# A four-layer convolution and attention kernel: its body is put into a block with another scheduler

## The chip, the cores and the metric

The kernel runs on one core of one Trainium2 chip. Every number is device time in microseconds (us). The metric is the median of the runs; before the change it is 3769.94 us, over 3 runs from 3769.51 to 3772.02. A separate profiled execution tells what each engine did. The engines are named as the profile names them: PE (TensorE, matmul), PEld (its weight load), DVE (VectorE), ACT (ScalarE), POOL (GpSimd) and SP (SyncE, whose queue issues the transfers here). Every engine works through its own queue in the order in which the program lists it. An instruction that waits holds up all that stand behind it on that engine.

## The reference, cut to what matters

The input is 4 images of 256 channels by 64 x 64, in float32. Four layers follow one another, each with a residual:

```
x = x + L0(gn(x))   # 3x3 convolution, group norm, relu -> xs; softmax attention over all 4096 positions
                    #   (theta, phi, g of 128 channels), 1x1 convolution, group norm * 0.1, + xs
x = x + L1(gn(x))   # linear attention: rmsnorm, q k v, softmax of q and k, 4 heads of 32, 1x1, rmsnorm
x = x + L2(gn(x))   # depthwise 3x3 and 1x1 convolutions whose weights are generated from pooled x
x = x + L3(gn(x))   # 1x1 convolution with a mixture of 4 expert weights, mixed by pooled x
```

`gn` is a group norm without weights. The full attention of L0 is the largest part: a 4096 x 4096 table of exponentials per image.

## The kernel before, in words

One function, `conv_preact_fast`, records all instructions for all four images. Tiles come from pools: the work pool has 7 buffers of 128 x 1024 (`k4`), 5 of 128 x 512 (`k2`), 3 of `pr`, 4 of `u`; the PSUM pool has 4 banks for general use (`bank`), 2 for `pf` and 2 for `acc` (`py` and `pss`). A scheduler then takes the recorded instructions and sets their order on each engine, and with it which instructions of different stages lie beside each other. No order is written out by hand, except that the stages are recorded in the sequence of lines 656 to 669: filter transform, then for each image b the tail of image b-1, the convolution of image b+1, the attention of image b and the projection of image b+1. The last image's tail is recorded last, with nothing beside it.

The stages and their lines:

- `convolve` (307 to 355): the 3x3 convolution in a transformed domain. DVE makes the transformed rows and columns (`down`, `across`, into `ra` and `v`), PE multiplies by filters that SP loads into `u` from DRAM (ps_conv, line 325), DVE adds the results up in `big`. It starts with the group norm of the image (`normalise`, bn_stats at 286) and ends with `smoothed` (296 to 305): statistics, then relu on ACT (304), whose result is also stored in DRAM as `xs_d`.
- `project` (358 to 372): theta and phi (ps_tp, 365) and g (ps_g, 370) for 8 chunks of 512 columns. ACT moves the first two from PSUM to `tpg` (366), DVE the third (372).
- `attend` (374 to 413): 8 tiles q0 to q7 of 512 columns. For each of 16 steps m there are two matmuls pf (387), two exponentials on ACT into `pr` (388), two matmuls py (397) and one addition `tot` on DVE (400 and 402, in the helper at 62). At the end of a tile DVE sums the halves of `tot` (`inv`, 404), PE adds over the partitions (pss, 407), DVE takes the reciprocal (408) and multiplies (`yt`, 412), and SP stores `yt` to `y_d` (413).
- `nonlocal_out` (416 to 442): it loads `yt` again, multiplies by a 1x1 weight (ps_wy, 425), takes a group norm, loads `xs` and `xr`, and adds them (438 and 439, in the helper at 65), with statistics for the next norm (441).
- `linear_attention` (445 to 525) has two loops of 8 chunks. The first goes from a normalised copy `xg` and its squares (453, 455) through a sum of squares (ps_ss, 460), ps_qkv (471), exponentials (473), a softmax of q (478 to 480) and a transpose (483) to a running product (ps_ctx, 487). Line 494 stands between the loops. The second goes from ps_o (510) through an rmsnorm (511 to 518) and transposes (522) to an addition into `big` (523) with statistics (524).
- `generated` (530 to 599): ps_h (545) pools a hidden layer, DVE makes the weights `dk` and `pk`, then 64 tap operations `dw` (587) on DVE, ps_pw (595) and the addition into `big` (597).
- `mixed` (602 to 651): mixes the expert weights, then ps_ex (647) and the store of the output.

All of these work on one `big` and one `xp`. What can lie beside a stage of the tail or of the convolution is therefore the attention of another image: it needs `tpg` alone. At the end of the kernel a check of the value range decides on a branch to a general version (`conv_preact_general`), which isn't taken here.

## Time and profile before

| | us |
|---|---|
| median of 3 runs | 3769.94 |
| lowest, highest | 3769.51, 3772.02 |
| profiled execution, its own time | 3772.22 |
| profiled execution, span from first to last instruction | 3770.4 |
| TensorE clock granted in it, mean | 0.912 |
| images 1 to 3, from the end of q6 of one image to that of the next | 907 |
| last tail, with nothing beside it, from the last pss to the end | 423 |

In the tables of stretches, a line gives a stretch of time (from:to in us), its length, and for each engine its busy time with the number of instructions. A float32 matmul shows as two instructions there, and counts as one in the text. The granted clock is 1.00 where the throttle lets TensorE run at full speed. The "chain" is followed back from the last instruction, at each step to what released it. By its lines it runs through pf (20%) and py (20%), ps_conv (9%) and the taps `dw` (8%).

### The profile page before, as it was taken

What the parts mean: (1) busy time and instruction counts of PE and PEld (TensorE: products, weight loads), DVE (VectorE), ACT (ScalarE), POOL (GpSimd) and SP (SyncE); (2) the same over time, 40 slices, a digit from 0 to 9 for tenths busy, and PEclk for the clock granted to TensorE, in tenths of its full rate; (3) what the DMA queues carried; (4) which work ended last, traced back from release to release, by engine and by line L of the source; (5) the groups of instructions that cost most, each with busy time, mean ns of one, the idle gap of its engine ahead of it and who ended that gap; (6) DMA issues with size and microseconds to landing.
All of it is one profiled execution on the core that took longest, in us unless ns stands there. A gap on an engine that the chain in (4) does not pass through costs nothing.

```text
span 3770.4 us, 24367 instructions
## 1 busy us (share of the span) xinstructions
PE 3150.8 (84%) x8322; PEld 1498.2 (40%) x8322; DVE 2208.6 (59%) x2696; ACT 1125.4 (30%) x2111; POOL 88.9 (2%) x133
## 2 busy tenths in 40 slices
PE   4699999989956889998984879999897699967645
PEld 2254444445422334444531334445452244434412
DVE  8869344353697944436479773444567734452476
ACT  2122333335410033333540013333443033323220
POOL 0000000001000000000100000000010000000000
PEclk9899999999977999999996889999998799987667
DMA  5313000020012220001001230000101200020011
GB/s 184 124 35 104 24 6 3 9 73 1 1 52 80 64 90 3 6 20 59 1 26 54 80 117 3 6 9 23 51 1 40 83 6 6 9 67 6 0 31 51
DMA packets 84484, 151.20 MB, mean 40 GB/s; under 512 B 8960, under 2 KB 46592, under 8 KB 82176
## 3 DMA queue, kind: packets, MB, share of 16 engines
q1 hardware_dynamic: 84352, 149.57, 11.6%
q8 instruction: 68, 1.11, 0.1%
q14 instruction: 64, 0.52, 0.0%
HBM read 101.30 MB, written 48.23 MB: 40 GB/s over the span
## 4 chain that ended last, share of the span: by engine, by line
PE 66%; DVE 21%; issue 7%; ACT 3%; POOL 2%; DMA 0%; SPq 0%; POOLq 0%; ACTq 0%; DVEq 0%
PE pf L387 20%; PE py L397 20%; PE ps_conv L325 9%; DVE dw L65 8%; PE ps_ex L647 3%; PE ps_tp L365 3%; DVE big L65 3%; PE ps_qkv L471 2%; PE ps_h L545 2%; PE ps_g L370 1%; PE ps_wy L425 1%; DVE z L62 1%; ACT junk L515 1%; DVE st L598 1%; PE ps_o L510 1%
## 5 line engine op out<-in xcount | busy, mean ns | idle before, releaser
L388 ACT ACTIVATE pr<-pf 128x512 f32<-128x512 f32 x1024 | 604.6, 596 | 1437.8 <-PE pf L387 1105.9
L62 DVE TENSOR_TENSOR tot<-tot,pr 128x1024 f32<-128x1024 f32 x448 | 547.9, 1223 | 826.1 <-ACT pr L388 825.7
L387 PE MATMUL pf<-tpg 128*128 128x512 f32 x2048 | 989.3, 605 | 22.7 <-ACT pr L388 22.7
L397 PE MATMUL py<-pr,tpg 128*128 128x512 f32 x2048 | 976.9, 600 | 11.1 <-DVE ev L62 7.7
L387 PEld LDWEIGHTS pf<-tpg 128*128 128x128 f32 x2048 | 385.7, 193 | 508.8 <-issue 419.1
L397 PEld LDWEIGHTS py<-pr,tpg 128*128 128x128 f32 x2048 | 390.6, 193 | 489.4 <-issue 471.7
L325 PE MATMUL ps_conv<-v,u 128*128 128x512 f32 x768 | 351.1, 618 | 88.3 <-issue 48.5
L595 PE MATMUL ps_pw<-dw,pk 128*128 128x512 f32 x256 | 158.8, 773 | 194.8 <-DVE dw L65 170.6
L65 DVE SCALAR_TENSOR_TENSOR dw<-xp,dk,dw 128x1008 f32<-128x1008 f32 (+1 forms) x256 | 309.9, 1262 | 6.4 <-ACT dw L582 6.2
L325 PEld LDWEIGHTS ps_conv<-v,u 128*128 128x128 f32 x768 | 151.2, 199 | 285.1 <-issue 239.4
L471 PE MATMUL ps_qkv<-wqkv_s,xg 128*128 128x384 f32 x512 | 190.3, 529 | 0.0
L595 PEld LDWEIGHTS ps_pw<-dw,pk 128*128 128x128 f32 x256 | 60.3, 250 | 292.0 <-DVE dw L65 187.4
L328 ACT COPY one<-ps_conv 128x512 f32<-128x512 f32 x48 | 28.1, 586 | 364.9 <-PE ps_conv L325 352.3
L408 DVE RECIPROCAL inv<-pss 128x512 f32<-128x512 f32 x32 | 107.4, 3356 | 42.9 <-PE pss L407 42.9
L471 PEld LDWEIGHTS ps_qkv<-wqkv_s,xg 128*128 128x128 f32 x512 | 103.6, 208 | 68.1 <-issue 16.0
L62 DVE TENSOR_TENSOR s<-sq 128x512 f32<-128x512 f32 x32 | 22.2, 692 | 182.5 <-ACT sq L455 182.5
L365 PE MATMUL ps_tp<-big,wtpg_s 128*128 128x512 f32 x256 | 118.9, 605 | 4.1 <-ACT big L304 4.1
L647 PE MATMUL ps_ex<-big,wm 128*128 128x512 f32 x256 | 119.2, 626 | 0.0
L202 PE MATMUL pm<-mv,avg 128*128 128x2 f32 x48 | 10.1, 279 | 127.8 <-DVE mv L198 96.6
L62 DVE TENSOR_TENSOR v<-ra 128x1024 f32<-128x1024 f32 x96 | 114.4, 1218 | 0.3
L62 DVE TENSOR_TENSOR tpg<-ps_g,bg_s 128x512 f32<-128x512 f32 x32 | 22.1, 690 | 118.1 <-PE ps_g L370 118.1
L138 POOL TENSOR_TENSOR rstd<-rstd,half 128x2 f32<-128x2 f32 x24 | 18.6, 773 | 3057.7 <-DVE rstd L212 3057.7
(176 smaller groups left out, 2679.3 us busy)
## 6 DMA issues: line engine op xcount, KB each, us to landing
u<-filters SPq DMA_DIRECT2D x192, 128.0 KB, 2.3
xp<-in_x_dram SPq DMA_DIRECT2D x16, 1024.0 KB, 5.1
xs_d<-big SPq DMA_DIRECT2D x32, 512.0 KB, 3.0
xs<-xs_d SPq DMA_DIRECT2D x32, 512.0 KB, 6.1
xr<-in_x_dram SPq DMA_DIRECT2D x32, 512.0 KB, 5.3
out_dram<-res SPq DMA_DIRECT2D x64, 256.0 KB, 2.0
y_d<-yt SPq DMA_DIRECT2D x32, 256.0 KB, 2.0
yt<-y_d SPq DMA_DIRECT2D x32, 256.0 KB, 2.9
```

What stands on the lines that cost most here:

```text
L62: nc.vector.tensor_tensor(o, a, b, op)
L65: nc.vector.scalar_tensor_tensor(o, a, s, b, op0, op1)
L325: nc.tensor.matmul(ps, u[:, h, :], vs[k][:, bass.ts(h, 512)], start=(h == 0), stop=(h == NH - 1))
L365: nc.tensor.matmul(ps, wtpg_s[:, h, k, :], big[:, h, cols], start=(h == 0), stop=(h == NH - 1))
L387: nc.tensor.matmul(pf, phi[:, bass.ts(2 * m + s, P)], theta[:, cols], start=True, stop=True)
L388: nc.scalar.activation(pr[:, bass.ts(s, 512)], pf, AF.Exp)
L397: nc.tensor.matmul(py, g[:, bass.ts(2 * m + s, P)], pr[:, bass.ts(s, 512)], start=(m == 0 and s == 0), stop=(m == NM - 1 and s == 1))
L408: nc.vector.reciprocal(inv, pss)
L471: nc.tensor.matmul(ps[:, 0:3 * HID], xg[:, h, bass.ts(j, P)], wqkv_s[:, h, :], start=(h == 0), stop=(h == NH - 1))
L545: nc.tensor.matmul(ps[0:2 * R, :], w1n[:, h, :], big[:, h, bass.ts(c, 512)], start=(h == 0), stop=(h == NH - 1))
L595: nc.tensor.matmul(ps, pk[:, h * NH * P + oh * P:h * NH * P + (oh + 1) * P], dw[h][:, bass.ts(s, 512)], start=(h == 0), stop=(h == NH - 1))
L647: nc.tensor.matmul(ps[oh], wm[:, h, bass.ts(oh, P)], big[:, h, cols], start=(h == 0), stop=(h == NH - 1))
```

## The change

The call of the fast body is put into a block that is asked to schedule by stepping through a model of the chip's timeline. The default scheduler orders everything outside of it, as it did for the whole before. The pools, their buffers, the recorded instructions and the sequence in which they are recorded stay the same. What changes is the order on each engine's queue and which buffer of a pool a tile gets.

```
@@ -1175,7 +1175,8 @@
     B = args[0].shape[0]
     gp = ctx.enter_context(tc.tile_pool(name="guard", bufs=1))
     guard = gp.tile([P, 2, B * NQ + 1], F32, name="guard")
-    conv_preact_fast(tc, guard, *args)
+    with tc.block(name="fast", schedule_with_timeline_sim=True):
+        conv_preact_fast(tc, guard, *args)
 
 
     fit = gp.tile([P, 2, B * NQ + 1], F32, name="fit")
```

In the built programs the orders of PE, DVE, ACT and SP differ over most of their length. In the steady part of the attention the order on PE was pf pf py py and is pf py pf py.

More of the change, by code (lines that the diff above doesn't have):

```diff
@@ L1177, in conv_preact_kernel @@
     guard = gp.tile([P, 2, B * NQ + 1], F32, name="guard")
-    conv_preact_fast(tc, guard, *args)
+    with tc.block(name="fast", schedule_with_timeline_sim=True):
+        conv_preact_fast(tc, guard, *args)
     fit = gp.tile([P, 2, B * NQ + 1], F32, name="fit")
```

## The prediction

> **What bounds the kernel now.** I read the page first (span, busy shares, the chain that ended last), then cut the period of one image into its stages and asked for the busy time of each engine in each, then the same for the last image, whose tail runs with nothing beside it, and last two short timelines.

> ```profile
> span 3770.4 us, 24367 instructions
> PE 3150.8 (84%) x8322; PEld 1498.2 (40%) x8322; DVE 2208.6 (59%) x2696; ACT 1125.4 (30%) x2111; POOL 88.9 (2%) x133
> PE 66%; DVE 21%; issue 7%; ACT 3%; POOL 2%; DMA 0%; SPq 0%; POOLq 0%; ACTq 0%; DVEq 0%
> ```

> TensorE carries two thirds of the chain, VectorE a fifth: the bound changes by stage. The busy table by stretch (columns: stretch, length, busy us and count of PE, PEld, DVE, ACT, POOL, granted clock, DMA share, GB/s), second image:

> ```profile
> 711.80:767.80 56.00, 56.00 (x131) 24.47 (x131) 23.72 (x20) 20.76 (x36) 0.00 (x0) 1.00 0.03 10
> 767.80:816.30 48.50, 48.50 (x197) 28.41 (x197) 18.68 (x24) 18.45 (x30) 0.00 (x0) 1.00 0.14 44
> 816.30:865.20 48.90, 31.21 (x73) 13.83 (x71) 41.28 (x64) 12.28 (x20) 1.45 (x3) 0.79 0.29 97
> 865.20:949.00 83.80, 83.56 (x346) 51.86 (x345) 27.90 (x49) 50.52 (x109) 9.35 (x15) 1.00 0.00 1
> 949.00:1026.20 77.20, 70.60 (x247) 39.46 (x247) 59.91 (x88) 28.75 (x92) 8.75 (x9) 1.00 0.00 1
> 1026.20:1150.90 124.70, 72.11 (x138) 25.34 (x137) 108.30 (x120) 26.52 (x39) 0.00 (x0) 0.78 0.17 57
> 1198.20:1319.10 120.90, 90.17 (x195) 38.76 (x195) 113.06 (x125) 11.74 (x16) 0.70 (x1) 0.86 0.19 58
> 1319.10:1393.80 74.70, 61.16 (x147) 28.15 (x148) 34.04 (x47) 25.75 (x37) 0.70 (x1) 0.89 0.28 111
> ```

> In order: the last attention tile q7 of an image (65 matmuls, 56.00/65 = 0.861 us each, PE full); `project` and ps_wy (full); the residual of `nonlocal_out` (PE idles 17.7 us, DVE 84% busy); the first loop of `linear_attention` (full); its second loop; `generated` (DVE-bound); `convolve` (DVE-bound); the rest of attention tiles q1 and q2. The same stages of the last image, bare:

> ```profile
> 3368.90:3410.80 41.90, 2.07 (x9) 1.85 (x9) 34.19 (x57) 3.15 (x4) 1.45 (x3) 0.54 0.34 113
> 3410.80:3514.10 103.30, 87.02 (x292) 57.57 (x292) 18.75 (x41) 43.62 (x95) 8.44 (x15) 0.76 0.00 1
> 3514.10:3596.80 82.70, 41.73 (x135) 32.97 (x136) 44.91 (x73) 14.56 (x65) 8.75 (x9) 0.64 0.00 0
> 3596.80:3719.10 122.30, 59.66 (x102) 19.90 (x102) 101.01 (x108) 23.10 (x32) 0.00 (x0) 0.70 0.08 24
> ```

> To see here: the second loop (82.7 against 77.2) and `generated` (122.3 against 124.7) take about as long bare as with attention matmuls between. Attention put there costs almost nothing; put where PE is full, it costs 0.861 us a matmul. One chunk of the first loop, from ps_qkv to ps_qkv, with attention between (9.96 us) and bare (12.30 us):

> ```profile
> 897.82 5.41 PE L471 MATMUL ps_qkv<-wqkv_s,xg 128*128 128x384 f32 x16
> 907.78 5.41 PE L471 MATMUL ps_qkv<-wqkv_s,xg 128*128 128x384 f32 x16
> 3426.51 7.29 PE L471 MATMUL ps_qkv<-wqkv_s,xg 128*128 128x384 f32 x16
> 3438.81 6.67 PE L471 MATMUL ps_qkv<-wqkv_s,xg 128*128 128x384 f32 x12
> ```

> **The change part by part.** No instruction of the computation is added or removed; only the order on each engine's queue changes, and the queues run in order. I counted the attention matmuls (pf and py) by stage in the instruction orders of the two built programs, per image. Before: project and ps_wy 0, residual 31, first loop 25, second loop 56, `generated` 18, up to ps_ex 6: 136. After: 24, 62, 48, 0, 0, 0: 134. So 80 matmuls leave stages that hide them, and 78 of these go into the stages ahead, and 24 ps_tp and 48 ps_g matmuls of `project` move up between q7's.

> Working, us per image, second and third image (batches 1 and 2):
> - q7, project, ps_wy: before 56.0 + 48.5 = 104.5, full. After, PE alone: 56.0 + 24 x 0.861 (ps_tp) + 48 x 0.22 (ps_g; from 48.5 less 42 x 0.861 over 56) + 24 x 0.861 + 16 x 0.861 = 121.8. Bounds +17 (nothing waits) and +22 (py waits at two tile ends). Taken: +18.5.
> - Residual: 48.9 before. After, PE 62 x 0.861 + 0.9 (pss) = 54.3 is the floor. DVE has 34.2 bare, plus 13 tot adds x 1.22, inv 0.7 and the reciprocal 3.36: 54.2; the bare chain has 7.7 idle besides: 62. On PE six py (5.2) now stand between the reciprocal and the group norm's second matmul, and everything of the first loop waits for that: upper end 68. Taken 62, for the stage is nearest to the bare row: +13.
> - First loop: without its 25 attention matmuls it is 83.8 - 21.5 = 62.3 on PE, 7.8 a chunk. After, the chunks hold 12, 10, 10, 9, 5, 1, 0, 0 of the 48 (the last one follows). Five PE-bound chunks: 5 x 7.8 + 46 x 0.861 = 78.6; three chain-bound ones at 9.96 to 12.30, taken 11.2: 33.6; end 4.1 (83.8 - 8 x 9.96): 116. Floor is PE alone, 62.3 + 41.3 = 103.6; upper end 120. +32.
> - Second loop bare: 82.7 by the last image, less if the 13.4 us of tot adds that leave DVE were in its way (64). Taken 81, nearer to the row that is the same work: +4.
> - `generated`: 122.3 for 124.7: -2.4. DVE now finishes pk 30 taps later, so ps_pw starts later, but DVE, which bounds the stage, has the same list to do. Up to mixed's first ps_ex 12.3 for 18.9: -6.6. ps_ex at the lower clock 31 for 28.4: +2. `convolve` has no attention in either order, and DVE bounds it: 0 (-3 to +3).
> - From convolve's end to the end of q2: before 74.7 with 61 of PE, because py and ps_tp wait behind smoothing. After, 22 pf and py are placed in that gap, so some 24 us to the first ps_tp as before, then the rest of the stage's 62.1 of PE (60 attention matmuls, 8 ps_tp, 16 ps_g), 62.1 - 20.7 = 41.4: 66, -9 (-12 where smoothing is quicker, -5 where it is not).
> Sum +51.5. The last interleaved image (batch 3) has no convolve, and its gap before ps_ex is bare already: 18.5 + 13 + 32 + 4 - 2 - 2 = +63.5.

> Elsewhere. Steady tiles (56.0): yt now stands behind the next tile's first tot on DVE. The order's waits say that the next py waits for the count that the reciprocal raises, not for yt; 0, upper end 24 tiles x 1.22 = 29. First convolve: 16 bn_stats of the next image (0.6 each) now stand ahead of the last t adds: +5 of these 10. The last tail has the same PE order: 0. On SP's queue the y_d and xs transfers change places with u loads, which run four ahead: 0 to +10, taken 0. POOL's order is unchanged but for memsets at the start.

> Total 2 x 51.5 + 63.5 + 5 = 171.5. On the profiled execution (span 3770.4, own time 3772.2) that makes a span of 3942; the median of the runs is 2.3 under that execution's time, so **3941**.

> A rule that speaks against this order: the granted clock was 1.00 in the filled second loop and 0.64 in the bare one, where ps_o's mean went from 379 to 588 ns. [...]

> **The rivals.**
> 1. Floors (3827): the chains don't matter, each stage ends at PE's own sum. 17 + 5.4 + 20 - 9 - 2.4 - 6.6 - 12 = +12.4 twice, and +31 for the last: +56. For: PE is at 100% in many stretches. Against: the residual and three bare chunks have chains that the last image shows.
> 2. New waits (3985): pf and py alternate one by one and the pools' releases decide; yt's 29 and some 15 more in `project` inside q7, where each ps_tp needs a bank freed by ACT after pf has read phi. Against: pf runs two to eight ahead.
> 3. Not slower (3770 or below): the bare stages shorten. The last image's bare stages from the second loop to ps_ex hold 135 us of PE at a clock of 0.64 to 0.90; at 1.00 they would hold some 36 less (41.7 x 0.36, 59.7 x 0.30, 31.4 x 0.10). If all that lay on the path, with the three chunks at 9.96 (-4), the residual at its floor (-8) and q2 at its best (-3), each image gets 51 back and the change costs nothing. It decides from a clock of about 1.00 in the bare stages. Against: the clock sank in every stretch where PE idled (0.54 to 0.79).
> 4. That nothing changes: excluded, the orders differ on every engine.

> **How the numbers follow.** Main case 0.62, rival 1 0.16, rival 2 0.14, rival 3 0.08. The range from 3860 to 4005 leaves out rival 3 and half of rival 1, and holds the upper ends of single terms. Within 0.2% is what a measurement of this kernel can't tell from no change; slower 0.92, same 0.02, faster 0.06.

> **What would show it.** Right: stretches of q7 of 87 us; about 62 from the last ps_wy to the first ps_ss; a first loop near 116; a second loop and `generated` without pf or py, near 81 and 122, at a clock under 0.8; steady tiles still 56.0; PE's busy time about the same and its idle time some 170 us longer. Wrong: if the bare stages shrink by more than 10 us each, or steady tiles lengthen, or if `convolve` or the first 430 us move by more than 15.

## The result and the profile after

The changed kernel takes 3959.79 us (median of 3 runs, 3959.01 to 3964.73), the kernel before 3769.94. The ratio is 1.0505, with a 95% interval of 1.0484 to 1.0525: slower, 19 us above the 3941 forecast. The profiled execution has a span of 3957.2 us, 186.8 more than before. The page of the changed kernel, in the parts that answer to those of before:

```profile
span 3957.2 us, 24425 instructions
PE 3174.8 (80%) x8322; PEld 1528.6 (39%) x8322; DVE 2213.0 (56%) x2696; ACT 1133.7 (29%) x2111; POOL 86.6 (2%) x133
PE 28%; DVE 11%; issue 2%; ACT 2%; POOL 1%; DMA 0%; SPq 0%; ACTq 0%; POOLq 0%; DVEq 0%
```

TensorE is busy 24 us longer than before, VectorE as long as before. So 163 of the 187 us are time in which TensorE stands still. (The chain's shares add up to under a half here, so nothing is read from it.) The busy table by stretch, second image, cut at the same landmarks as before (columns: stretch, length, busy us and count of PE, PEld, DVE, ACT, POOL, granted clock, DMA share, GB/s):

```profile
711.70:799.00 87.30, 87.30 (x276) 44.45 (x275) 27.78 (x28) 28.24 (x48) 0.00 (x0) 1.00 0.04 13
799.00:833.50 34.50, 34.50 (x81) 14.95 (x80) 20.99 (x23) 16.55 (x29) 0.00 (x0) 1.00 0.15 46
833.50:904.60 71.10, 59.75 (x136) 25.76 (x135) 54.32 (x74) 20.89 (x35) 1.45 (x3) 0.93 0.19 67
904.60:1014.60 110.00, 104.73 (x389) 61.67 (x387) 31.10 (x51) 57.90 (x120) 8.44 (x15) 0.98 0.00 1
1014.60:1096.40 81.80, 40.75 (x136) 32.12 (x137) 45.29 (x73) 14.58 (x65) 8.75 (x9) 0.68 0.00 0
1096.40:1226.20 129.80, 53.05 (x102) 17.95 (x101) 107.11 (x118) 23.19 (x32) 0.00 (x0) 0.69 0.16 54
1273.70:1386.80 113.10, 87.54 (x196) 37.70 (x195) 109.99 (x122) 11.72 (x16) 0.69 (x1) 0.91 0.19 61
1386.80:1461.10 74.30, 65.96 (x174) 30.94 (x174) 36.02 (x51) 27.52 (x40) 0.70 (x1) 0.93 0.30 113
```

In order: q7 with the early part of `project` and 12 attention matmuls; the rest up to the last ps_wy; the residual; the first loop; the second loop; `generated`; `convolve`; and the rest of q2. The residual has 136 TensorE rows where it had 73, and the first loop 389 where it had 346. The second loop fell from 247 to 136 and `generated` from 138 to 102, at a clock of 0.68 and 0.69. So the attention matmuls went where the orders of the two programs said, and the two stages that are left bare take 81.8 and 129.8 us, against 77.2 and 124.7 with the matmuls in them. A steady tile is still 56.0 us (pss at 430.8, 486.8, 542.8).

Time by stage, from the landmarks in the two traces, against the terms of the sum (us, second / third image):

| stage | before | after | measured | forecast |
|---|---|---|---|---|
| q7, project, ps_wy | 104.5 / 105.4 | 121.7 / 121.7 | +17.2 / +16.3 | +18.5 |
| residual, to the first ps_ss | 48.8 / 48.4 | 71.1 / 70.7 | +22.3 / +22.3 | +13 |
| first loop, to the first ps_o | 84.0 / 83.9 | 110.0 / 109.9 | +26.0 / +26.0 | +32 |
| second loop, to the first ps_h | 77.0 / 77.0 | 81.8 / 81.9 | +4.8 / +4.9 | +4 |
| generated, to the last ps_pw | 124.7 / 123.8 | 129.8 / 129.8 | +5.1 / +6.0 | -2.4 |
| to the first ps_ex | 18.9 / 20.3 | 16.4 / 16.0 | -2.5 / -4.3 | -6.6 |
| ps_ex | 28.4 / 30.1 | 31.1 / 31.3 | +2.7 / +1.2 | +2 |
| convolve and on to the end of q2 | 195.6 / 194.8 | 187.4 / 187.1 | -8.2 / -7.7 | -9 |
| sum | 682.0 / 683.8 | 749.4 / 748.4 | +67.4 / +64.6 | +51.5 |
| last interleaved image, q6 to q2 | 541.6 | 611.8 | +70.2 | +63.5 |
| up to q6 of the first image | 711.8 | 711.7 | -0.1 | +5 |
| last tail, q6 to the last ps_ex | 471.7 | 456.4 | -15.3 | 0 |

### The profile page after: what moved, and what is told of

It reads as the page before. It is cut to its first block, busy times and chain, and to the rows that moved or that the text cites. A ratio compares the mean times of both kernels' runs of the same rounds, so it can differ in the third digit from the quotient of the medians.

```text
span 3957.2 us, 24425 instructions
## 1 busy us (share of the span) xinstructions
PE 3174.8 (80%) x8322; PEld 1528.6 (39%) x8322; DVE 2213.0 (56%) x2696; ACT 1133.7 (29%) x2111; POOL 86.6 (2%) x133
## 5 line engine op out<-in xcount | busy, mean ns | idle before, releaser
L397 PE MATMUL py<-pr,tpg 128*128 128x512 f32 x2048 | 1035.5, 601 | 26.0 <-DVE gm L204 13.3
L387 PE MATMUL pf<-tpg 128*128 128x512 f32 x2048 | 1038.2, 598 | 20.7 <-ACT pr L388 20.7
L595 PE MATMUL ps_pw<-dw,pk 128*128 128x512 f32 x256 | 144.1, 723 | 286.4 <-DVE pk L65 234.8
L471 PE MATMUL ps_qkv<-wqkv_s,xg 128*128 128x384 f32 x512 | 190.8, 523 | 0.0
L522 PE MATMUL ps_zt<-ident,z 128*128 128x128 f32 x256 | 62.2, 424 | 144.5 <-DVE z L62 144.5
L471 PEld LDWEIGHTS ps_qkv<-wqkv_s,xg 128*128 128x128 f32 x512 | 101.9, 204 | 71.2 <-issue 20.9
L515 ACT ACTIVATE junk<-z 128x256 f32<-128x256 f32 x128 | 52.0, 407 | 227.4 <-DVE z L62 227.4
L522 PEld LDWEIGHTS ps_zt<-ident,z 128*128 128x128 f32 x256 | 50.2, 223 | 162.0 <-issue 143.0
L510 PE MATMUL ps_o<-w,xp 128*128 128x256 f32 x256 | 102.2, 571 | 1.9 <-ACT w L501 1.9
```

The costliest lines, as they stand in the source:

```text
L387: nc.tensor.matmul(pf, phi[:, bass.ts(2 * m + s, P)], theta[:, cols], start=True, stop=True)
L397: nc.tensor.matmul(py, g[:, bass.ts(2 * m + s, P)], pr[:, bass.ts(s, 512)], start=(m == 0 and s == 0), stop=(m == NM - 1 and s == 1))
L471: nc.tensor.matmul(ps[:, 0:3 * HID], xg[:, h, bass.ts(j, P)], wqkv_s[:, h, :], start=(h == 0), stop=(h == NH - 1))
L510: nc.tensor.matmul(ps[:, j, :], qT[:, bass.ts(4 * c + 2 * s + j, P)], w2, start=True, stop=True)
L522: nc.tensor.transpose(pt[:, bass.ts(j, P)], z[:, j, bass.ts(h, P)], ident)
L595: nc.tensor.matmul(ps, pk[:, h * NH * P + oh * P:h * NH * P + (oh + 1) * P], dw[h][:, bass.ts(s, 512)], start=(h == 0), stop=(h == NH - 1))
```

## The experiments

Two questions were open. Is it the place of the attention matmuls that costs, or are it waits that the new orders of VectorE and ScalarE bring? And why does the new order spend them early and then have none for the second loop?

### What a matmul costs in each stage, by itself

Both runs add to the changed kernel 56 matmuls of pf's shape per image in images 0 to 2. Nobody reads their product; every other result is as before.

```
 second loop, after the chunk's last ps_o                first loop, after the chunk's last ps_ctx
+    more = bank("more")                                 +    more = bank("more")
+    with tc.issue_after(last.ins):                      +    with tc.issue_after(last.ins):
+        for _ in range(7):                              +        for _ in range(7):
+            nc.tensor.matmul(more, ident, ...)          +            nc.tensor.matmul(more, ident, ...)
```

(`issue_after` sets an order on the engine's queue and adds no wait.)

> The changed kernel with extra work that nobody reads: in each chunk of the second loop of images 0 to 2, behind its last ps_o, seven more matmuls of pf's shape (128x512), 56 for an image, 168 in all, 168 x 0.861 = 145 us of TensorE at full clock. This measures by itself what a matmul costs in the stage that the change left bare. Theory P: nothing, since TensorE was busy 41 of 82 us there and is at 28.6 us of work at full clock: 28.6 + 48.2 = 77 us fit into the stage, so it stays between 75 and 86 us and the kernel between 3945 and 3975. Rival (work added to the stage lengthens its chain): up to 145 us, 4105.

> The changed kernel with the same extra work that nobody reads as in the run on the second loop (seven matmuls of 128x512 a chunk, 56 for an image, 168 in all, 145 us at full clock), but in the first loop of images 0 to 2, behind each chunk's last ps_ctx. Theory P: the stage is full there, so a matmul costs its 0.861 us, but for the last three chunks, which had room for some 3 us each: 48 - 8 = 40 us for an image, 3960 + 120 = 4080, between 4050 and 4110; the same work cost nothing in the second loop. Rival (a matmul costs the same wherever it stands): 3941, as there.

Measured: 3941.39 us with the work in the second loop (ratio to the kernel before 1.0460, 1.0443 to 1.0478), 18 us less than without it; and 4096.53 us with it in the first loop (1.0860, 1.0844 to 1.0877), 137 us more. The second loop with the added work, and the first loop with it, second image, from the busy tables of the two runs:

```profile
1017.50:1095.10 77.60, 72.41 (x249) 42.34 (x250) 43.25 (x73) 14.83 (x65) 8.75 (x9) 0.96 0.00 1
```

```profile
906.30:1062.20 155.90, 150.97 (x501) 82.06 (x499) 31.10 (x51) 58.07 (x120) 8.44 (x15) 1.00 0.00 1
```

In the second loop TensorE goes from 40.75 to 72.41 us of work, the granted clock from 0.68 to 0.96, and the stage gets shorter, from 81.8 to 77.6 us: at the higher clock its own ps_o and transposes are faster (means of 408 and 273 ns for 571 and 424; in the kernel before, 379 and 276 in the filled stage at a clock of 1.00, 588 and 424 in the bare one at 0.64), and the added ones lie in its gaps. The kernel lies 4 us below the range that theory P gave, since I had not forecast that the work would gain anything. In the first loop the same 56 matmuls cost 155.9 - 110.0 = 45.9 us, 0.82 us each. So the same work costs less than nothing in one stage and its full duration in the other; the last three chunks of the first loop had hardly any of the room that I gave them. This is theory P, that the place sets the price, in its plainest form.

### The counts by stage put back, or taken over

The first run holds the attention matmuls of images 1 to 3 in the changed kernel, so that each stage has the count of before. The second makes the mirror in the kernel before.

```
+PLAN = (('W', 31), ('s0', 3), ..., ('o0', 7), ..., ('h0', 4), ...)   # behind which matmul, how many
 ...
+    with held(b):      # tc.issue_after(the matmul that PLAN names)
         nc.tensor.matmul(pf, ...)
```

```
+PLAN = (('W0', 24), ('W', 62), ('s0', 12), ('s1', 10), ('s2', 10), ('s3', 9), ('s4', 5), ('s5', 2))
         for q in range(NQ):
+          with tc.high_priority() if (b > 0 and q < 2) else nullcontext():
```

> The changed kernel, its scheduler kept, but each early attention matmul (pf, py) of images 1 to 3 is queued on TensorE behind a named matmul of the other image's tail, so that the counts by stage become the ones of before: 31 in the residual, 25 in the first loop, 56 in the second loop, 18 in generated, 6 up to ps_ex (changed: 24 ahead of the last ps_wy, 62, 48, 0, 0, 0). Theory P (the place of these matmuls is the loss): the three interleaved images give back what they lost, 67.4 + 64.6 + 69.1 = 201 us, and the last tail keeps its 15 us of gain: 3960 - 201 = 3759, between 3745 and 3790. Rival W (the orders that the new scheduler gave VectorE and ScalarE, and the waits in them, are the loss): 3900 or more, since those orders stay. Half each would be 3860. Profile under P: second loop near 77 us with the clock near 1.00, residual near 49.

> The mirror: the kernel before, its default scheduler kept, but the first two attention tiles of images 1 to 3 are given priority over the tail, and their matmuls are queued so that they stand where the changed kernel has them: 24 among the ps_wy, 62 in the residual, 50 in the first loop, none from the second loop to ps_ex. Theory P: the three images lose 201 us as in the changed kernel, and the last tail stays as before: 3770 + 201 = 3971, between 3940 and 3995 (it lies a little above the changed kernel, which has 15 us of gain in its last tail). Rival W: the default order of VectorE and ScalarE is kept, so 3770 to 3820.

Measured: 3885.01 us (1.0299, 1.0282 to 1.0316), and 4089.20 (1.0845, 1.0827 to 1.0863). Neither theory was right: the first run gives back only 75 us, the mirror loses 319 and not 201. In the mirror the residual takes 94.2 us and the first loop 125.8, against 71.1 and 110.0 in the changed kernel with the same counts. The stages of the first run tell more. The residual is back at 51.8 us and q7 to the last ps_wy at 106.6, but the first loop takes 108.5 with its 25 matmuls (84.0 in the kernel before, also with 25), and `generated` 142.9 with its 18. TensorE's work in one chunk of the first loop, kernel before:

```profile
887.86 5.41 PE L471 MATMUL ps_qkv<-wqkv_s,xg 128*128 128x384 f32 x16
893.10 0.83 PE L487 MATMUL ps_ctx<-v,qk 128*128 128x129 f32 x6
893.77 1.02 PE L387 MATMUL pf<-tpg 128*128 128x512 f32 x2
894.63 0.39 PE L487 MATMUL ps_ctx<-v,qk 128*128 128x129 f32 x2
894.86 1.88 PE L397 MATMUL py<-pr,tpg 128*128 128x512 f32 x4
896.57 0.60 PE L483 MATMUL ps_qt<-ident,qk 128*128 128x128 f32 x4
```

and with the counts put back, but behind ps_ss (start, length; in brackets the idle time ahead and what ended it):

```profile
912.21 1.54 PE L487 MATMUL ps_qkv<-wqkv_s,xg 128*128 128x384 f32 x4
913.58 1.88 PE L413 MATMUL py<-pr,tpg 128*128 128x512 f32 x4
915.30 1.02 PE L402 MATMUL pf<-tpg 128*128 128x512 f32 x2
916.15 4.03 PE L487 MATMUL ps_qkv<-wqkv_s,xg 128*128 128x384 f32 x12
920.02 0.83 PE L503 MATMUL ps_ctx<-v,qk 128*128 128x129 f32 x6
921.01 0.49 PE L503 MATMUL ps_ctx<-v,qk 128*128 128x129 f32 x2 [0.15 <-ACT v L490]
922.58 0.63 PE L499 MATMUL ps_qt<-ident,qk 128*128 128x128 f32 x4 [1.08 <-DVE qk L63]
```

In the kernel before three matmuls stand between ps_ctx and ps_qt, just where TensorE would wait for VectorE's softmax of q, and no wait is left. Three matmuls some microseconds earlier in the same chunk delay ps_qkv by 2.6 us, and the wait of 1.08 us for `qk` stays. In `generated` of the same run, 15 of them stand among the ps_h or right behind them, ahead of ps_pool, on which `pk` and then every ps_pw depend. From the first ps_h to ps_pool 29.6 us pass, against 18.1 in the changed kernel and 15.7 in the kernel before, and the stage is 13 us longer than in the changed kernel. TensorE's long wait for `pk` doesn't come from these matmuls: it is as long in the changed kernel, where none stand in this stage (the run, then the changed kernel; total, times, longest):

```profile
PE ps_pw L611 <- DVE pk L66: 58.2, 1, 58.2
```

```profile
PE ps_pw L595 <- DVE pk L65: 58.7, 1, 58.7
```

In the kernel before the first ps_pw starts 19 us behind ps_pool, in the other two 59 to 60: that is VectorE's new order, in which `pk` comes late.

So a count by stage is too coarse. A matmul was free here in a gap of the chain, not in a stage that has gaps: with 25 of them in both, the first loop took 84.0 us in the kernel before and 108.5 in this run.

### TensorE's and VectorE's whole order exchanged

The next four runs therefore take over orders whole: a table of the other kernel's order, as runs of (first, count) in recorded sequence, tied to the engine's queue with no wait added.

```
+PE_ORDER = ((0, 199), (298, 2), (199, 1), (300, 14), ...)     # 4354 matmuls
+DVE_ORDER = (...)                                             # 2660 instructions, in the last two runs
+    row = [made[k] for at, n in order for k in range(at, at + n)]
+    for a, b in zip(row, row[1:]):
+        tc.add_manual_dep(b, a.name, <no sync>, reason="order")
```

> The changed kernel with every matmul of TensorE's queue, all 4354, put into exactly the order that the kernel before has (issue order only, no wait added); the timeline scheduler then orders VectorE, ScalarE and the transfers around it. The run that moved only counts by stage gave back 75 of 201 us, and its first loop (108.5 us) still held waits of ps_qt for VectorE: its 25 attention matmuls stood behind ps_ss and not, as in the kernel before, in the gap between ps_ctx and ps_qt. Theory P2 (the place to the single matmul is the loss): 3755 to 3785, the first loop near 84 us and full. Rival W (the orders of VectorE and ScalarE): like that run, 3860 to 3900.

> The mirror: the kernel before, default scheduler, with all 4354 matmuls of TensorE's queue in exactly the order of the changed kernel; the default scheduler orders VectorE, ScalarE and the transfers around it. Theory P2: 3960 to 3985 (the changed kernel's time, and up to 15 us more where the last tail is without its gain), residual near 71, first loop near 110, second loop near 82 us. Rival W: 3850 or less.

> The changed kernel with both TensorE's order (4354 matmuls) and VectorE's order (2660 instructions) of the kernel before; ScalarE and the transfers are left to the timeline scheduler. With TensorE's order alone it took 3808, 37 us above the kernel before, 10 of them in generated in each image. Theory V (the rest is VectorE's order, which no longer fitted TensorE's): 3760 to 3780. Rival (the rest is on ScalarE or the transfers): 3800 or more.

> The mirror: the kernel before with both TensorE's and VectorE's order of the changed kernel. With TensorE's order alone it took 4070, 110 us above the changed kernel (residual 81 to 85 us for 71, the stretch behind convolve 91 for 74). Theory V: 3945 to 3980, the changed kernel's time. Rival (ScalarE or the transfers): 4030 or more.

| kernel | us | ratio to the kernel before |
|---|---|---|
| changed, TensorE's order of before | 3807.96 | 1.0093 (1.0076 to 1.0110) |
| changed, TensorE's and VectorE's of before | 3782.67 | 1.0030 (1.0019 to 1.0040) |
| before, TensorE's order of the changed | 4069.65 | 1.0790 (1.0772 to 1.0808) |
| before, TensorE's and VectorE's of the changed | 4004.67 | 1.0624 (1.0608 to 1.0640) |

TensorE's order alone gives back 152 of the 190 us, twice what the counts gave; with the matmuls in their gaps the first loop is full again:

```profile
875.10:960.70 85.60, 84.72 (x346) 52.75 (x347) 27.87 (x48) 49.97 (x109) 8.45 (x15) 1.00 0.00 1
```

VectorE's order gives back 25 more. The other way round, TensorE's order makes all of the loss and 110 us besides, and VectorE's order takes 65 of these away: the residual goes from 81.1 to 70.9 us, the changed kernel's value. So rival W is right in this: an order on one engine cost extra where the other engine's queue wasn't ordered for it, 65 us in this case. None of the four met its range: the runs with TensorE's order alone lie 23 and 85 us above that of P2, the last two 3 and 25 us above that of V. What is left, 12 us one way and 45 the other, has to be on ScalarE, POOL, the transfers or the buffers that the tiles got; no run parts these. Of the 45, 12 lie before the end of the first image's q6, 12 and 11 in the next two images, mostly behind `convolve` (84 us for 74), 13 in the last tail, and -3 in the third image. Only the last tail has runs of its own.

### The last tail

It was forecast at 0, since TensorE's order in it is the same, and became 15 us shorter, nearly all in the first loop of `linear_attention`. The prediction shows its busy line of before (103.30 us, TensorE 87.02 at a clock of 0.76). After:

```profile
3612.50:3701.20 88.70, 75.60 (x292) 49.35 (x292) 19.38 (x41) 43.49 (x95) 8.44 (x15) 0.88 0.00 1
```

The same 292 rows of TensorE took 87.02 us and then 75.60, at another clock. What differs is ScalarE's order: before, the two `xg` and `sq` of the next chunk stood one by one between the exponentials of this one, after, they stand ahead of most of them. Two runs of the kernel before test that, one with the last tail in a block, one with priority for these two lines.

```
+    with tc.block(name="last", schedule_with_timeline_sim=True):
         tail(B - 1)
```

```
+    with tc.high_priority() if b == 3 else nullcontext():
         xg ... activation(xg[:, h, :], ...); activation(sq, xg, AF.Square)
```

> The kernel before with only its last tail, which has nothing beside it, in a block of the timeline scheduler. In the changed kernel this tail took 409 us against 423 of before with the same order on TensorE, nearly all of it in the first loop of linear_attention (88.6 against 103.3 us, granted clock 0.88 against 0.76). Theory A (the order on ScalarE does it: xg and sq of the next chunk stand ahead of most of this chunk's exponentials): 3770 - 15 = 3755, plus 0 to 5 for the block's border. Rival (a chance of the clock's phase, carried in from the tiles ahead, which were a little shorter in the changed kernel): 3770, the first loop near 103.

> The kernel before with xg and sq of the last image's first loop given priority, so that on ScalarE they stand ahead of most of the chunk's exponentials, nearly as the timeline scheduler put them; nothing else of the program is touched. In the run with the last tail alone in a timeline block the first loop fell from 103.3 to 94.2 us, and the block's border took 9.2 us back. Theory A (ScalarE's order does it): first loop 88 to 95 us, kernel 3755 to 3763. Rival (it is not ScalarE's order): 3770.

Measured: the block gives 3770.06 (0.9996, 0.9987 to 1.0006): its first loop is 94.2 us instead of 103.3, but from the end of q6 to the last ps_wy it takes 87.0 instead of 77.8. At the block's border every load of `yt` is issued behind the last tile's store, and the first ps_wy waits 7.8 us for one. The priority gives 3760.95 (0.9972, 0.9961 to 0.9982):

```profile
3410.50:3503.60 93.10, 80.65 (x291) 52.46 (x291) 19.38 (x41) 43.61 (x95) 8.44 (x15) 0.81 0.00 1
```

Its loop is 10.2 us shorter and the kernel 10 us, and in its profile TensorE and VectorE work through the whole kernel in the same order as before: ScalarE's order is shown as the cause of two thirds of the 15 us. The block's run, at 3770, has the time that the rival forecast, but not the loop near 103 that went with it. The other runs' last tails settle the rival, that the shorter loop is a chance of the clock. In all of them TensorE's and VectorE's orders in this loop are those of the kernel before. The five programs that also keep its order on ScalarE take 100.0 to 103.3 us for the loop, the nine in which the two `xg` stand together 87.9 to 94.2. Programs of one kind differ by up to 6 us, so the last third of the 15 us lies within that spread. The waits tell how small the first step is. TensorE's wait for the softmax of q in the kernel before and in the changed one (total, times, longest):

```profile
PE ps_qt L483 <- DVE qk L62: 12.1, 8, 2.9
```

```profile
PE ps_qt L483 <- DVE qk L62: 10.2, 8, 2.4
```

2 us less waiting there, and 11 us less time in the matmuls, at a clock of 0.88 for 0.76.

### Why there is nothing left for the second loop

In both programs, 134 to 136 attention matmuls stand ahead of the end of `convolve`: two tiles (128) and the start of a third. Something stops the third. An attention tile ends by taking two tiles of `k2` (`junk` and `yt`), and `convolve`, recorded ahead of it, takes `k2` tiles for `one` to its very end. The trace shows the first early tile held there. In the kernel before its reciprocal starts at 963.8 us, but its `junk` and `yt` run 350 us later, `junk` right behind the last `one`:

```profile
1313.99 0.59 ACT L328 COPY one<-ps_conv 128x512 f32<-128x512 f32 x1 [6.59 <-PE ps_conv L325]
1314.48 0.63 ACT L410 ACTIVATE junk<-inv 128x512 f32<-128x512 f32 x1
1327.88 0.63 DVE L62 TENSOR_TENSOR yt<-py,inv 128x512 f32<-128x512 f32 x1
```

In the changed kernel the reciprocal starts at 884.5, the last `one` at 1381.8, `junk` at 1382.3 and `yt` at 1383.9. Until its `yt` has read it, the first tile's py holds one of the two `acc` buffers, and the second tile's py has the other, so the second tile can't take its pss; that runs at 1329.4 in the one and 1391.2 in the other. Two runs write junk and yt over the tile's own `inv` instead, one of the kernel before, one of the changed kernel.

```
-            junk = k2("junk")
-            nc.scalar.activation(junk, inv, AF.Copy, accum_out=...)
-            yt = k2("yt")
-            tt(yt, py, inv, ALU.mult)
-            nc.sync.dma_start(out=y_d[b, :, cols], in_=yt)
+            nc.scalar.activation(inv, inv, AF.Copy, accum_out=...)
+            tt(inv, py, inv, ALU.mult)
+            nc.sync.dma_start(out=y_d[b, :, cols], in_=inv)
```

> The kernel before with one change of buffers: the accumulating copy and y (junk, yt) of an attention tile are written over its own inv and no longer take two tiles of the k2 buffers that the tail and convolve share. In both orders only 134 to 136 attention matmuls, two tiles and the start of a third, stand ahead of convolve's end. Theory L (that limit is yt, whose k2 tile comes in recorded order behind the last tile of convolve): with it gone the order has 14 for 6 ahead of ps_ex, and 46 more between ps_ex and the end of convolve, where TensorE has room. 46 x 0.861 = 40 us leave the stretch behind convolve in images 1 and 2, less 46 x 0.305 = 14 us of tot adds in a VectorE-bound stage and 5 ahead of ps_ex: -20 twice, -10 for the last: 3720, between 3690 and 3750. Rival (VectorE is the bound there, so nothing is gained): 3760 to 3790.

> The changed kernel with the same change of buffers. Under theory L the timeline scheduler spent its 134 matmuls early and then had none left for the second loop and generated; with the limit gone its order has them everywhere: per image some 85 up to the last residual matmul, 82 in the first loop, 112 in the second, 62 in generated, 38 ahead of ps_ex, 40 around ps_ex and 66 in convolve, some 480 of 512. TensorE's full-clock work for one image and its tail is 448 (attention) + some 290 = 740 us, against 907 of before and 973 of the changed kernel, and VectorE's some 560. Theory L: 800 to 860 an image, so 3960 - 2 x 130 - 90 = 3610, between 3450 and 3700. Rival (the in-order queues wait on the exponentials wherever attention stands in a tail's chain, or VectorE's 1.22 us adds delay the chain): 3770 or more.

Measured: 3657.90 us with the default scheduler (0.9698, 0.9682 to 0.9715), and 3499.02 us with the timeline scheduler (0.9277, 0.9261 to 0.9292): 271 us less than the kernel before, 461 less than the changed kernel. The page of the latter, and its first loop, second loop, `generated` and `convolve`:

```profile
span 3497.0 us, 24215 instructions
PE 3100.9 (89%) x8322; PEld 1483.5 (42%) x8322; DVE 2195.8 (63%) x2696; ACT 1126.1 (32%) x2111; POOL 87.8 (3%) x133
```

```profile
889.90:1027.70 137.80, 137.80 (x475) 76.85 (x474) 50.27 (x67) 70.67 (x142) 8.43 (x15) 1.00 0.01 2
1027.70:1140.40 112.70, 112.70 (x350) 59.00 (x348) 78.28 (x104) 46.48 (x121) 8.75 (x9) 1.00 0.01 5
1140.40:1291.60 151.20, 119.78 (x229) 45.52 (x228) 129.73 (x139) 38.88 (x65) 0.00 (x0) 0.84 0.15 49
1390.70:1530.80 140.10, 140.10 (x328) 62.11 (x327) 124.70 (x134) 27.27 (x47) 0.00 (x0) 1.00 0.19 60
```

(The residual ahead of them is 66.8 us.) Each of these four stages is longer than in either kernel, and the image is shorter: from the last ps_wy of one image to that of the next, 907 us before and 973 in the changed kernel have become 809 and 806, of which TensorE works 773 at a clock of 0.97. Theory L holds: the limit was the buffer. With the default scheduler and the new buffers the second early tile's pss runs at 1164.8 us instead of 1329.4. (That the buffers of a tag go out in the recorded sequence is my reading of it; shown is that the limit goes when these two tiles leave `k2`.) With the default scheduler the gain was 114 us, twice the forecast and beyond its range: the period fell by 41 us an image, which is all of 46 x 0.861 = 40; the 14 us that I took off for VectorE's additions were not lost.

This turns the meaning of the change round. With enough attention to lay beside the tail, the timeline scheduler is 159 us better than the default one (3499 against 3658). With two tiles of it, it is 190 us worse, because it uses them as soon as TensorE can take them, and TensorE can take them first where each one costs 0.86 us.

## Why the prediction was right, and where it was off

The direction and the main mechanism, the place of the attention matmuls, were right, and so was the size: 3960 for 3941. The size owes something to luck: the three interleaved images lost 36 us more than forecast, and the last tail and the start gave 20 of them back. By its own steps:

- **The counts by stage carry the loss.** Right as a forecast: the three images lost 202 us for 166 forecast. As a cause it was too coarse, which only the runs showed: the counts put back gave 75 us, TensorE's whole order 152, and VectorE's order 25 more.
- **q7, project, ps_wy (+18.5).** +17: nothing waited, the stretches are full at a clock of 1.00.
- **Residual (+13).** This step failed: +22, beyond the upper end of 68 us. VectorE's busy time was forecast at 54.2 and measured at 54.3. The miss is in "the bare chain has 7.7 idle besides". In the bare tail 6.8 us pass from the group norm's first matmul to the first ps_ss; here 21.6. VectorE's reciprocal stands ahead of the copy of `gm`, then six py ahead of pv:

```profile
882.99 0.28 PE L202 MATMUL pm<-mv,avg 128*128 128x2 f32 x2
884.52 3.35 DVE L408 RECIPROCAL inv<-pss 128x512 f32<-128x512 f32 x1
887.78 0.10 DVE L204 COPY gm<-pm 128x2 f32<-128x2 f32 x1
887.92 8.00 PE L397 MATMUL py<-pr,tpg 128*128 128x512 f32 x12 [4.65 <-DVE gm L204]
895.75 0.28 PE L210 MATMUL pv<-ev,avg 128*128 128x2 f32 x2
```

  I had named these six py and priced them at 5.2; behind TensorE's wait of 4.65 us the clock was 0.67 and they took 8.0, and ten more pf and py stand between pv and ps_ss.
- **First loop (+32).** +26, between the floor of 103.6 and the upper end of 120.
- **Second loop (+4).** +5. What the prediction held against this order, the lower clock of the bare stage, came: 0.68, with 40.75 us of TensorE's work in a stage of 81.8. The 28.6 us that the run on this loop was forecast with, as the stage's work at full clock, is shown by no run: in the filled stage of the kernel before (949.0 to 1026.2, clock 1.00) ps_o and ps_zt hold 15.1 + 8.6 = 23.7 us. The run with useless work in the gaps puts a number on the clock: at 0.96 the stage takes 77.6, so the lost clock is worth about 4 us of it, as an estimate from these two times.
- **generated (-2.4) and on to ps_ex (-6.6).** Wrong by some 8 and 3 us. I took the bare row of the last image, 122.3, but that image has no successor: in the second and third, 12 bn_stats of the next image's norm, 0.68 us each, stand in VectorE's list of this stage (118 instructions, 107.1 us busy, against 108 and 100.9 in the last). The third tail, which has no next image to normalise either, took exactly 122.3. These bn_stats make the forecast wrong, but they don't make the stage 5 us longer: the kernel before has 11 of them there too. Of the 5 us, 2.4 lie between the first ps_h and ps_pool (18.1 for 15.7), and the cause of the rest stays open.
- **convolve (0) and behind it (-9).** -8 in sum, but by luck, for both terms were wrong. `convolve` was forecast at 0 and took 113.1 us for 120.9, -8. The stretch behind it was forecast at 66 and took 74.3 for 74.7: its TensorE work shrank as forecast (42.3 us from the first ps_tp, for 41.4), but the way to the first ps_tp, taken as 24 as before, took 32.0. What `convolve` gained was lost there again.
- **Steady tiles (0) and the first 430 us (+5).** 56.0 still, and nothing lost up to q6 of the first image (-0.1).
- **Last tail (0).** This step failed: -15, by ScalarE's order and the clock that came with it. "The same PE order: 0" forgot that the other queues are ordered anew too.

The rivals: new waits (3985) had a part that is real, the residual's end and the 38 us that TensorE's order alone doesn't give back. The floors (3827) missed those chains. The third rival, which needed a clock of about 1.00 in the bare stages, met 0.68 and 0.69. What no rival held is that the limit on the early matmuls is a buffer, and that the change is a gain of 159 us where it is gone.

## What to carry to other kernels

Work that is to fill the gaps of another stage has its price by the place, to the single instruction: the same 56 matmuls cost 46 us in a stage that was full and made another stage 4 us shorter. So before judging a scheduler, ask how much filling work it has and what ends it; here two buffers of a shared tag ended it after two tiles, and freeing them took 114 us off the kernel before and 461 off the changed one. And a new order on one queue should be judged together with the others': TensorE's order alone, moved into the other program, cost 110 us more than in its own.
